# A four-layer hybrid network on one core: filter scaling and filtered copies moved to ScalarE, and the first scan unit written out by halves

## Chip, core and metric

The kernel is one program on one core of a Trainium2 chip. The metric is the device time of one execution in microseconds (us). The kernel before takes 3038.94 us, the median of three runs (3038.47 to 3039.41).

The engines are TensorE (PE in the profile; its weight loads are PEld), VectorE (DVE), ScalarE (ACT), GpSimd (POOL) and SyncE (SP), which issues most of the DMAs. Matmul results go to PSUM[...]. Everything here is float32; a 512-column product is two records of TensorE.

## What is computed

The input x has 8 images of 128 channels and 16 x 16 points, so 256 positions an image and 2048 positions in all. Four layers follow one another:

```python
x = x + adder2d(group_norm(x), W)                 # layer 0: minus the sum of |w - x| over 3x3 taps
# layer 1: three selective scans (forward, backward, sliced) over the positions
u, z  = split(layer_norm(x) @ in_proj.T)          # 256 channels each
uc    = silu(causal_conv1d(u, w4) + b)            # four taps
dt, Bm, Cm = split(uc @ xproj.T)                  # 8, 16 and 16 columns
delta = softplus(dt @ dtproj.T + db)
h_t   = exp(delta * A) * h_(t-1) + delta * uc * Bm   # 16 states a channel
y     = sum over states of h * Cm + uc * D
# ... attention between the three y, a gate with z, two 3x3 convolutions, + x
# layer 2: attention of one head, then a mixture of 8 experts (top 2)
# layer 3: 8 layers of linear attention and feed-forward, a tanh; then the spectral layer:
U_plus, U_minus = causal convolution of u (and of u with alternating sign) with 16 filters phi
out   = sum over k of sigma_k**0.25 * (U_plus[k] @ M_plus[k] + U_minus[k] @ M_minus[k])  + 3 taps of u @ M_u
```

The spectral layer is computed for four lengths of the sequence, weighted by a one-hot vector.

## The kernel before, in words

**Layer 0** (`adder_layer`, from line 303). For each of 128 filters and nine taps VectorE (line 419, 415) or ScalarE (421) makes a 128x2048 tile d, and TensorE sums it over channels with one-column selectors. The filters come in four groups of 32. After the last, `sums` (428) goes by four DMAs a group (430) to `total`, and four operations on VectorE (434) write X, the activations of layer 1, in four blocks of 512 positions. The tiles `x`, `w`, `pad`, `sh`, `sums` and `total` stand in one SBUF pool, "l0". The pools of layer 1 are laid over it, so a tile of layer 1 waits for what last used the bytes beneath it.

**Layer 1** (`_scans`, from 502). The work is cut into 12 units, each a pair of images (one block of 512 positions) and one of the three branches. A unit is prepared and then scanned. The preparation gives uc, delta, du = delta * uc and, through DRAM, the rows of B and C, each spread over the 128 partitions by DMA (`chunk`, 722). Channels come in two halves, h = 0 and 1. A scan runs over 16 states of a unit. For each state r and half: ScalarE makes the decay da (`decays`, 746; tiles da0 to da2 in three PSUM banks, number 2r + h modulo 3), GpSimd makes dbu = du * B (`inputs`, 736), VectorE scans (825) and multiplies both halves by C (836; for states 1 and 8 of a unit GpSimd does it, 834), and TensorE adds up the states in PSUM (acc). ScalarE first copies C to PSUM (`rows_of_c`, 741).

PSUM in this stage: three banks for da, one each with the tags "s", "f" and "cs", and two with the tag "acc".

The order of the loop over the states is written by hand (`tc.manual_schedule`, 808): the preparation of the next units (`prepare`, 646) and the work of `beside` (769) are mixed in by small steps. `first_unit` (668) prepares unit 0, when nothing else can run beside it, and stands outside of the hand-written order: a scheduler sorts its instructions. It normalises the block, projects it (two halves, pu), filters each half on TensorE with four products with diagonal matrices (pconv), makes the sigmoid from Exp, Ln and Exp, projects (pp), and for each half computes softplus: Abs and Relu, Exp, 1 + e to PSUM, Ln, and three operations on VectorE. Then du (713), the first dbu (739, on VectorE) and the first decays follow, and the first two steps of unit 1's preparation.

**Layers 2 and 3** (`performer_layer`, 1014). Four blocks of 512 positions go through 8 layers each; their steps are mixed by a table (`ORDER`) in a hand-written order. Blocks 0 and 1 run ahead of the others through layer 2 (`AHEAD`), beside the end of layer 1. `_block` (1393) is one block's way; at 1432 it adds the feed-forward to the state H, and `_squares` (1366) then squares H on ScalarE. Two sets of ScalarE tables alternate here (one with Ln and Exp, one with Gelu).

**The spectral layer.** `Spectral.__init__` (1662), called ahead of layer 2, loads the filter matrices T (16 of 128 x 258 columns) and scales all of them by sigma**0.25 with one operation on GpSimd (1673). `spectral_layer` (1711) takes two filters a step, in eight steps. VectorE makes the weighted matrices m (1706, 1708; two buffers, loaded by DMA); their sum and difference are me (1754 on VectorE, 1755 on GpSimd; two buffers). TensorE filters: 16 products p (two records each, three PSUM banks), each copied to ug by VectorE and ScalarE in turn:

```python
if n_evac % 2:
    nc.scalar.copy(dst, p4)          # line 1766
else:
    nc.vector.tensor_copy(dst, p4)   # line 1768
```

20 products g of me and ug then add to the result. All products are issued by the helper at line 279, all activations of layers 2 and 3 by the one at 1097, so groups are told apart by their tiles.

Of the kernel before, what the change touches and what calls it, by code (L numbers as in the profile page):

```python
# [16 lines left out]
P = 128  # L17
# [285 lines left out]
def adder_layer(E):  # L303
# [8 lines left out]
    with ExitStack() as ctx:  # L312
        p = ctx.enter_context(tc.tile_pool(name="l0", bufs=1))
        accp = ctx.enter_context(tc.tile_pool(name="l0acc", bufs=3))
        absp = ctx.enter_context(tc.tile_pool(name="l0abs", bufs=4))
        po = ctx.enter_context(tc.tile_pool(name="l0po", bufs=2, space=PSUM))
        ps = ctx.enter_context(tc.tile_pool(name="l0ps", bufs=2, space=PSUM))

        x = p.tile([P, B, L], F32, tag="x", name="x0")
        for b in range(0, B, 2):  # L320
            nc.sync.dma_start(x[:, b : b + 2, :], E.dram["x"][b : b + 2].rearrange("b c s -> c b s"))
        E.load_shared()
# [77 lines left out]


        sums = p.tile([P, NG, BLK], F32, tag="sums", name="sums")
        total = p.tile([P, NBLK, BLK], F32, tag="total", name="total")
        for g in range(NG):
            out = po.tile([P, BLK], F32, tag="o", name="o")
            for r in range(FG):
# [95 lines left out]
def _scans(E, ctx, F):  # L502
# [113 lines left out]
            E.mm(pp, w_x[:, k, h, :], uc[:, h, :], start=h == 0, stop=h == 1)  # L616
        return pp

    def softplus(k, s, h, proj, d, e, r, tag, gen):

        pd = ps.tile([P, UT], F32, tag=tag, name="pd")
        E.mm(pd, w_dt[:, k, h * P : (h + 1) * P], proj[0:DTR, :])
        yield 1
        yield LATER
        db = E.v("db" + s, h)
        nc.scalar.activation(e, pd, AF.Abs, bias=db)
        nc.scalar.activation(d, pd, AF.Relu, bias=db)
        yield LATER
        nc.scalar.activation(e, e, AF.Exp, scale=-1.0)
        one_e = ps.tile([P, UT], F32, tag=tag, name="one_e")  # L630
        nc.scalar.activation(one_e, e, AF.Identity, bias=E.ones[:, 0:1])
        yield LATER
        nc.vector.scalar_tensor_tensor(e, one_e, -1.0, e, ALU.add, ALU.subtract)
        nc.scalar.activation(r, one_e, AF.Ln)
        gen.tensor_sub(r, r, e)
        gen.tensor_add(d, d, r)

    def tiles():
        uc, delta, du = (two.tile([P, 2, UT], F32, tag=n, name=n) for n in ("uc", "delta", "du"))
# [6 lines left out]
    def prepare(k, s, p, got):  # L646
        new, pre, sig, proj = tiles()
        uc, delta = new["uc"], new["delta"]
        for h in range(2):
            pc = ps.tile([P, UB, L], F32, tag="s", name="pconv")  # L650
            yield from convolution(k, s, h, us[p], pc)
            yield LATER
            biased(s, h, pc, pre[:, h, :])
        yield from sigmoid(sig, pre)
        nc.gpsimd.tensor_mul(uc, pre, sig)
        yield LATER
        pp = projections(k, uc, proj, "s")
        yield 2
        yield LATER
        nc.scalar.copy(proj, pp)  # L660
        nc.sync.dma_start(new["rows"], proj[DTR:, :])
        got.update(new)
        for h in range(2):
            yield from softplus(k, s, h, proj, delta[:, h, :], pre[:, h, :], sig[:, h, :], "s", nc.gpsimd)
        yield LATER
        nc.gpsimd.tensor_mul(new["du"], delta, uc)

    def first_unit(k, s, p, got):

        src = E.X[:, blk(p)]  # L670
        pxc = ps.tile([P, UT], F32, tag="s", name="xc1")
        E.mm(pxc, E.center, src)
        rstd = one.tile([P, UT], F32, tag="ln_rstd", name="ln_rstd")
        nc.scalar.activation(rstd, pxc, AF.Square)
        var = ps.tile([P, UT], F32, tag="f", name="var1")
        E.mm(var, E.mean, rstd)
        nc.scalar.activation(rstd, var, AF.Ln, bias=E.eps)
        nc.scalar.activation(rstd, rstd, AF.Exp, scale=-0.5)
        t = xn[p] = two.tile([P, UT], F32, tag="xn", name="xn1")
        nc.vector.tensor_mul(t, pxc, rstd)  # L680
        nc.vector.tensor_scalar(t, t, E.v("ln_w"), E.v("ln_b"), ALU.mult, ALU.add)
        us[p] = two.tile([P, 2, UT], F32, tag="u", name="u1")
        tags = ("f", "s")
        for h in range(2):
            pu = ps.tile([P, UT], F32, tag=tags[h], name="pu")
            E.mm(pu, E.w["in_proj"][:, h * P : (h + 1) * P], t)
            (nc.vector.tensor_copy if h else nc.scalar.copy)(us[p][:, h, :], pu)
        for j, b in enumerate(BRANCHES):
            nc.scalar.activation(neg_a[:, j, :], E.vs("A" + b), AF.Exp)
        nc.vector.tensor_scalar_mul(neg_a, neg_a, -1.0)  # L690
        for d in das:
            nc.vector.memset(d[:, :, 0:1], 0.0)
        new, pre, sig, proj = tiles()
        uc, delta = new["uc"], new["delta"]
        for h in range(2):
            pc = ps.tile([P, UB, L], F32, tag=tags[h], name="pconv")
            for _ in convolution(k, s, h, us[p], pc):
                pass
            biased(s, h, pc, pre[:, h, :])
            for _ in sigmoid(sig[:, h, :], pre[:, h, :]):  # L700
                pass
            nc.vector.tensor_mul(uc[:, h, :], pre[:, h, :], sig[:, h, :])
        nc.scalar.copy(proj, projections(k, uc, proj, "f"))
        nc.sync.dma_start(new["rows"], proj[DTR:, :])
        parts = [
            softplus(k, s, h, proj, delta[:, h, :], pre[:, h, :], sig[:, h, :], tags[h], nc.vector) for h in range(2)
        ]
        for part in parts:
            next(part)
        for part in parts:  # L710
            for _ in part:
                pass
        nc.vector.tensor_mul(new["du"], delta, uc)  # L713
        got.update(new)


    units = [(k, s, p) for p in range(NPAIRS) for k, s in enumerate(BRANCHES)]
# [15 lines left out]
        c, j = divmod(n, CN)  # L733
        return got[i][name, c][:, j, :]

    def inputs(r, gen=nc.gpsimd):
        if r < states:
            dbs[r] = three.tile([P, 2, UT], F32, tag="db", name="dbu")
            gen.tensor_tensor(dbs[r], got[r // NST]["du"], bc(row("bs", r), 1, 2), ALU.mult)  # L739

    def rows_of_c(r):
        if r < states and r % NST not in AWAY:
# [46 lines left out]
            if p < NPAIRS - 2:  # L789
                yield from gates(p + 2)  # L790

    first_unit(*units[0], got[0])
    for c in range(2):
        chunk("bs", 0, c)
        chunk("cs", NST, c)
    for g in range(3):
        decays(g)
    inputs(0, nc.vector)
    inputs(1)
    rows_of_c(0)  # L800
    acc = late = None
    room = 0
    other = _Chain(beside())
# [589 lines left out]
def _block(S):  # L1393
# [23 lines left out]
    for i in range(NL):  # L1417
        sq = yield from _attention(S, i, h, sq, u, sums)
        w = S.layers[i]
        yield from _state_norm(S, h, sq, u)  # L1420
        g = one.tile([P, 4, BLK], F32, tag="g", name="g3")
        for f in range(0, 4, 2):
            p1 = [bank(S, [P, BLK], "p1") for _ in range(2)]
            for n in range(2):
                S.mm(p1[n], w["w1"][:, (f + n) * P : (f + n + 1) * P], u)
            for n in range(2):
                act(S, g[:, f + n, :], p1[n], AF.Gelu, bias=S.v(f"b1{i}", f + n))
            yield
        p2 = bank(S, [P, BLK], "p2")
        for f in range(4):  # L1430
            S.mm(p2, w["w2"][:, f * P : (f + 1) * P], g[:, f, :], start=f == 0, stop=f == 3)
        nc.vector.scalar_tensor_tensor(h, p2, S.added[f"b2{i}"], h, ALU.add, ALU.add)
        if i == NL // 2 - 1:
            yield
            pz = bank(S, [LAT, BLK], "pz3")
            S.mm(pz, S.enc, h)
            z = S.many.tile([P, BLK], F32, tag="t", name="z3")[0:LAT]
            act(S, z, pz, AF.Gelu, bias=S.v("enc_b")[0:LAT, :])
            yield
            ph = bank(S, [P, BLK], "ph2")  # L1440
            S.mm(ph, S.w["dec"], z)
            nc.vector.tensor_scalar_add(h, ph, S.added["dec_b"])
        if i + 1 < NL:
            sq = _squares(S, h)
            yield
            if S.t == 0:
                yield from _weights_of(S, i + 1)
# [211 lines left out]
class Spectral:  # L1659


    def __init__(self, E, ctx):
# [7 lines left out]
        self.H = pool.tile([P, NT], F32, tag="H", name="H")  # L1670
        self.u = pool.tile([P, B, TAPS - 1 + L], F32, tag="u", name="u4")
        nc.gpsimd.memset(self.u[:, :, 0 : TAPS - 1], 0.0)
        nc.gpsimd.tensor_tensor(self.T, self.T, bc(E.sg[:, :], 2, TW), ALU.mult)


        soft = pool.tile([P, 1, 4], F32, tag="soft", name="soft")
# [7 lines left out]
        nc.vector.tensor_sub(hot, hot, soft)  # L1684
        nc.vector.tensor_add(hot, hot, soft)
        self.hot = hot[:, 0, :]

    def take(self, E, t, xn, pt, dst):

# [21 lines left out]
def spectral_layer(E, W, out):  # L1711
# [8 lines left out]
    with ExitStack() as ctx:  # L1720
# [24 lines left out]
            a = tile[:]  # L1745
            return bass.AP(a.tensor, a.offset + offset, [list(a.ap[0]), *([s, n] for s, n in dims)])

        n_evac = 0
        for step in range(NK // KG):
            m = W.load(E, two, step)  # L1750
            W.running(E, [m[:, i].rearrange("p k s e -> p (k s e)") for i in range(4)])
# [6 lines left out]
            for b in range(B):  # L1758
                for q in range(2):
                    p4 = pu.tile([P, KG, 2, HL], F32, tag="u", name="p4")  # L1760

                    taps = at(W.T, step * KG * TW + 1, (TW, KG), (HL + 1 - q, 2), (1, HL))
                    E.mm(p4, ut[:, 2 * b + q, :], taps)
                    dst = at(ug, b * L + q * HL, (2 * NT, KG), (NT + (-HL if q else HL), 2), (1, HL))
                    if n_evac % 2:
                        nc.scalar.copy(dst, p4)  # L1766
                    else:
                        nc.vector.tensor_copy(dst, p4)  # L1768
                    n_evac += 1
            for k in range(KG):  # L1770
                for s in range(2):
                    for j, (i, lo, hi, b0, b1) in enumerate(groups):
# [61 lines left out]
```

## Time and profile before

| | us |
|---|---|
| median of three runs | 3038.94 |
| the profiled execution's own time | 3037.75 |
| its span, first to last instruction | 3036.0 |
| layer 0 (to the last d product) | 0 to 964 |
| first unit (to the first scan, L825) | 964 to 1004.75 |
| scans | 1004.75 to about 1700 |
| layer 1's end, layers 2 and 3 | about 1700 to 2790 |
| spectral layer | 2790 to 3036 |

The granted TensorE clock was 0.986 over the span. A line of the timeline has the start, the busy time, the engine, the program line, the operation with its tiles (out<-in) and shapes, the count, and in brackets how long the engine stood before it and what released it. A line of the waits has who waited, for whom, the total, the times and the longest. A line of the windows has the stretch, its length, then busy time and count of PE, PEld, DVE, ACT and POOL, the clock, the DMA share and GB/s. Instructions that overlap in an engine's pipeline are merged into one line, and a busy time can run into the next start.

### The profile page before, as it was taken

Reading aid. Unit: us, or ns where it says so; the run is one execution under the profiler, and the core shown is the slowest. Engines: PE = TensorE matmul, PEld = TensorE weight load, DVE = VectorE, ACT = ScalarE, POOL = GpSimd, SP = SyncE. Lnnn points to the kernel's source line nnn. Section 1 sums busy time; section 2 is a strip of 40 time slices with the busy share of each in tenths; the row PEclk is TensorE's granted clock in tenths of the full one; section 3 lists DMA queues with packets and bytes.
Section 4 is the critical chain, followed back from the end, with each engine's and each line's share of the span. In section 5 each row is a group of like instructions: output and inputs, shape, how many; then the busy total and the mean of one; then the engine's idle time right before and its main releaser. Section 6 shows DMA issues by size and latency. Waiting matters only on the chain.

```text
span 3036.0 us, 41650 instructions
## 1 busy us (share of the span) xinstructions
PE 2850.0 (94%) x16314; PEld 1258.5 (41%) x16314; DVE 2468.0 (81%) x3440; ACT 2228.8 (73%) x2664; POOL 732.1 (24%) x442
## 2 busy tenths in 40 slices
PE   6999999999998787998998998999999999999999
PEld 2222222222222233443443454455555655654444
DVE  6999999999997899999899657887777787784321
ACT  5999999999997777778777424577778778676111
POOL 3000000000000699998999400000000000000100
PEclk9999999999999999999999999999999999999999
DMA  1000000000000544444443200000000000001100
GB/s 41 1 2 5 2 1 5 1 1 5 2 1 5 166 142 150 133 148 144 134 156 136 86 28 1 14 1 14 14 14 1 14 14 1 14 1 52 42 28 14
DMA packets 39192, 131.47 MB, mean 43 GB/s; under 512 B 7490, under 2 KB 10572, under 8 KB 37588
## 3 DMA queue, kind: packets, MB, share of 16 engines
q1 hardware_dynamic: 38564, 128.02, 12.6%
q8 instruction: 128, 2.10, 0.3%
q10 hardware_dynamic: 432, 0.79, 0.1%
q14 instruction: 68, 0.56, 0.1%
HBM read 125.91 MB, written 1.84 MB: 42 GB/s over the span
## 4 chain that ended last, share of the span: by engine, by line
PE 68%; DVE 16%; ACT 7%; POOL 5%; issue 3%; DMA 1%; SPq 0%; DVEq 0%; ACTq 0%; POOLq 0%
PE o L279 30%; PE p L279 8%; PE acc L279 5%; DVE st L825 4%; PE g L279 4%; PE conv L279 4%; POOL dbu L739 2%; PE pc L279 2%; PE var L279 2%; PE pf L279 2%; PE pq L279 2%; PE pconv L279 1%; PE pa L279 1%; PE pn L279 1%; PE px L1584 1%
## 5 line engine op out<-in xcount | busy, mean ns | idle before, releaser
L279 PE MATMUL o<-d,sel 128*32 128x512 f32 x8512 | 922.8, 593 | 7.6 <-DVE d L419 5.5
L421 ACT ACTIVATE d<-sh,w 128x2048 f32<-128x2048 f32 x472 | 899.6, 1993 | 29.9 <-PE o L279 23.3
L419 DVE TENSOR_SCALAR d<-sh,w 128x2048 f32<-128x2048 f32 x592 | 724.5, 1292 | 13.5 <-PE o L279 10.4
L739 POOL TENSOR_TENSOR dbu<-du,bs 128x1024 f32<-128x1024 f32 x191 | 447.1, 2366 | 973.2 <-DVE du L713 970.9
L279 PEld LDWEIGHTS o<-d,sel 128*32 128x32 f32 x8512 | 274.3, 110 | 655.3 <-issue 533.0
L825 DVE TENSOR_TENSOR_SCAN st<-da,dbu 128x512 f32<-128x512 f32 x384 | 446.1, 1207 | 17.2 <-POOL dbu L739 15.1
L279 PE MATMUL acc<-st,cst 128*128 128x512 f32 x768 | 375.9, 621 | 57.3 <-DVE st L836 57.1
L752 ACT ACTIVATE da<-delta,neg_a 128x510 f32<-128x510 f32 x384 | 256.8, 684 | 79.0 <-DVE st L825 77.8
L279 PEld LDWEIGHTS acc<-st,cst 128*128 128x128 f32 x768 | 144.7, 196 | 256.2 <-issue 141.7
L836 DVE TENSOR_TENSOR st<-st,pcs 128x1024 f32<-128x1024 f32 x168 | 205.2, 1222 | 18.0 <-ACT pcs L744 0.9
L415 DVE SCALAR_TENSOR_TENSOR d<-sh,w,d 128x2048 f32<-128x2048 f32 x88 | 206.7, 2349 | 1.9
L1312 POOL TENSOR_TENSOR lw<-lw,turn 128x640 f32<-128x640 f32 x8 | 10.1, 1257 | 679.2 <-DVE turn L1311 586.3
L1089 ACT ACT_TABLE_LOAD x134 | 171.9, 1283 | 2.5
L1766 ACT COPY ug<-p 128x512 f32<-128x512 f32 x64 | 37.5, 585 | 181.9 <-PE p L279 181.9
L744 ACT COPY pcs<-cs 128x512 f32<-128x512 f32 x168 | 97.7, 582 | 55.2 <-DVE st L836 48.6
L279 PE MATMUL conv<-pad,f 128*128 128x512 f32 x288 | 135.0, 596 | 0.9 <-ACT pad L987 0.5
L279 PE MATMUL p<-un,lw 128*128 128x512 f32 x256 | 123.7, 605 | 3.8 <-DVE un L1383 2.1
L279 PE MATMUL p<-T,H 128*128 128x512 f32 x256 | 115.4, 603 | 6.1 <-DVE ug L1768 5.1
L279 PE MATMUL p<-g,lw 128*128 128x512 f32 x256 | 116.4, 597 | 3.9 <-ACT g L1097 3.9
L279 PE MATMUL g<-ug,me 128*128 128x512 f32 (+1 forms) x320 | 111.9, 509 | 0.0
L1097 ACT ACTIVATE ex<-ex 128x352 f32<-128x352 f32 x128 | 62.4, 493 | 51.6 <-DVE ex L1577 50.3
L279 PE MATMUL pf<-lw,rk 128*128 128x352 f32 x256 | 97.2, 476 | 0.5 <-DVE ek L1527 0.3
(347 smaller groups left out, 3943.0 us busy)
## 6 DMA issues: line engine op xcount, KB each, us to landing
bs<-rows SPq DMA_DIRECT2D x96, 512.0 KB, 3.8
cs<-rows SPq DMA_DIRECT2D x96, 512.0 KB, 4.7
m<-in_Mphi SPq DMA_DIRECT2D x8, 1024.0 KB, 4.8
lw<-in_layers SPq DMA_DIRECT2D x8, 948.0 KB, 4.5
f<-in_fuse SPq DMA_DIRECT2D x2, 1152.0 KB, 7.9
T<-in_T SPq DMA_DIRECT2D x1, 2064.0 KB, 7.6
x<-in_x SPq DMA_DIRECT2D x4, 256.0 KB, 7.4
total<-sums SPq DMA_DIRECT2D x16, 64.0 KB, 2.0
```

Of the source, the lines that this page charges most:

```text
L279: self.nc.tensor.matmul(out, lhsT=lhsT, rhs=rhs, start=start, stop=stop)
L415: nc.vector.scalar_tensor_tensor(d, tap(k), wk, d, ALU.max, ALU.add)
L419: nc.vector.tensor_scalar(d, tap(k), wk, None, ALU.max)
L421: nc.scalar.activation(d, tap(k), AF.Abs, scale=-1.0, bias=wk)
L739: gen.tensor_tensor(dbs[r], got[r // NST]["du"], bc(row("bs", r), 1, 2), ALU.mult)
L744: nc.scalar.copy(pcs[r], row("cs", r))
L752: nc.scalar.activation(das[g % 3][:, :, 1:], d[:, :, 1:], AF.Exp, scale=a)
L825: nc.vector.tensor_tensor_scan(st[:, h, :], da, dbs[r][:, h, :], 0.0, ALU.mult, ALU.add)
L836: nc.vector.tensor_tensor(st, st, bc(pcs[r][:, :], 1, 2), ALU.mult)
L1089: S.tc.keep_in_program_order(S.nc.scalar.preload_act_table_set(name))
L1097: S.nc.scalar.activation(out, src, func, **kw)
L1766: nc.scalar.copy(dst, p4)
```

## The change

It has three parts.

1. **First unit.** `x` and `total` of layer 0 get a pool of their own, `l0last`. `first_unit` becomes a generator within a hand-written order. Half 1 is filtered on VectorE, straight from the PSUM bank of its projection, by one tensor_scalar and three scalar_tensor_tensor; half 0 stays on TensorE, and its sigmoid starts from PSUM (Exp with the bias `less`). 25 products of the identity with itself (`spare`, in bank "acc") are put between the products of the unit. The softplus has its maximum on VectorE and 1 + e in SBUF. du and the first dbu are made by halves. The copy of u for half 1 comes last.
2. **Filter matrices.** The operation on GpSimd goes. While block 0 runs through its 8 layers, ScalarE scales two of the 16 matrices a layer, right after line 1432.
3. **Filtered signals.** All copies of p to ug are ScalarE's.

```diff
-        x = p.tile([P, B, L], F32, tag="x", name="x0")
+        x = last.tile([P, B, L], F32, tag="x", name="x0")
...
-        total = p.tile([P, NBLK, BLK], F32, tag="total", name="total")
+        total = last.tile([P, NBLK, BLK], F32, tag="total", name="total")
...
-    def first_unit(k, s, p, got):
+    def first_unit(k, s, p, new, pre, sig, proj):
+        spare = ps.tile([P, P], F32, tag="acc", name="spare")
+        def meanwhile(n):
+            for _ in range(n):
+                E.mm(spare, ident, ident)
...
+        meanwhile(9)
         pxc = ps.tile([P, UT], F32, tag="s", name="xc1")
-        E.mm(pxc, E.center, src)
+        E.mm(pxc, E.center, E.X[:, blk(p)])
...
+        meanwhile(1)
         var = ps.tile([P, UT], F32, tag="f", name="var1")
...
+        meanwhile(8)
...
+        for h, tag in ((1, "s"), (0, "f")):
+            pus[h] = ps.tile([P, UT], F32, tag=tag, name="pu")
+            E.mm(pus[h], E.w["in_proj"][:, h * P : (h + 1) * P], t)
+        nc.scalar.copy(us[p][:, 0, :], pus[0])
+        nc.vector.tensor_scalar(p1, u1, E.v("cw" + s, 7), E.v("cb" + s, 1), ALU.mult, ALU.add)
+        for m in range(1, 4):
+            o = p1[:, :, m:]
+            nc.vector.scalar_tensor_tensor(o, u1[:, :, : L - m], E.v("cw" + s, 7 - m), o, ALU.mult, ALU.add)
+        meanwhile(2)
...
+        nc.scalar.activation(t, pc, AF.Exp, scale=-1.0, bias=less)
+        nc.vector.tensor_scalar_add(pre[:, 0, :], pc, E.v("cb" + s, 0))
...
+        meanwhile(1)
+        E.mm(pp, w_x[:, k, 1, :], uc[:, 1, :], start=True, stop=False)
+        meanwhile(3)
+        E.mm(pp, w_x[:, k, 0, :], uc[:, 0, :], start=False, stop=True)
+        nc.scalar.copy(proj, pp)
+        nc.sync.dma_start(new["rows"], proj[DTR:, :])
+        yield
+        meanwhile(1)
...
+        for h, (pd, d, e, r, one_e) in enumerate(halves):
+            nc.scalar.activation(e, pd, AF.Abs, bias=db)
+            nc.scalar.activation(e, e, AF.Exp, scale=-1.0)
+            nc.vector.tensor_scalar(d, pd, db, 0.0, ALU.add, ALU.max)
+        for pd, d, e, r, one_e in halves:
+            nc.vector.tensor_scalar_add(one_e, e, 1.0)
+            nc.scalar.activation(r, one_e, AF.Ln)
+            nc.vector.scalar_tensor_tensor(e, one_e, -1.0, e, ALU.add, ALU.subtract)
+        for h, (pd, d, e, r, one_e) in enumerate(halves):
+            nc.vector.tensor_sub(r, r, e)
+            nc.vector.tensor_add(d, d, r)
+            nc.vector.tensor_mul(new["du"][:, h, :], d, uc[:, h, :])
+            yield
+        nc.scalar.copy(us[p][:, 1, :], pus[1])
+        yield
...
+        for h in range(2):
+            next(first)
+            nc.vector.tensor_mul(dbs[0][:, h, :], new["du"][:, h, :], row("bs", 0))
+            decays(h)
+            if h == 0:
+                rows_of_c(0)
+        inputs(1)
+        next(first)
+        decays(2)
...
         nc.vector.scalar_tensor_tensor(h, p2, S.added[f"b2{i}"], h, ALU.add, ALU.add)
+        if S.t == 0:
+            for k in range(i * NK // NL, (i + 1) * NK // NL):
+                S.spectral.scale(S, k)
...
-        nc.gpsimd.tensor_tensor(self.T, self.T, bc(E.sg[:, :], 2, TW), ALU.mult)
...
+    def scale(self, E, k):
+        E.nc.scalar.activation(self.T[:, k, :], self.T[:, k, :], AF.Copy, scale=E.sg[:, k : k + 1])
...
-                    if n_evac % 2:
-                        nc.scalar.copy(dst, p4)
-                    else:
-                        nc.vector.tensor_copy(dst, p4)
-                    n_evac += 1
+                    nc.scalar.copy(dst, p4)
```

In the built program the order of the instructions on each engine differs from the one before in these three places, and otherwise by a few neighbouring products on TensorE that change places. On VectorE the scan of state 0, half 0, comes between the subtraction and the addition of half 1. On ScalarE the order there is: decay of half 0, the copy of C, decay of half 1, the copy of u for half 1, and the decays for state 1, half 0 and half 1, and for state 2, half 0; then the bias of unit 1's first filtered half (pre), and only then the decay for state 2, half 1.

## The prediction

> **What bounds the kernel now.** I read the page first, for the engine that is never idle.
>
> ```profile
> PE 2850.0 (94%) x16314; PEld 1258.5 (41%) x16314; DVE 2468.0 (81%) x3440; ACT 2228.8 (73%) x2664; POOL 732.1 (24%) x442
> ```
>
> TensorE (PE) is busy for 94% of 3036.0 us, so a gain has to come from the few places where it stands, or from the scan stage (about 1005 to 1700), where VectorE is the busy one. The change touches three places, so I took the timeline of each. First the start of the scans (columns: start, busy time, engine, line, operation, and in brackets the idle time before it and what ended it):
>
> ```profile
> 967.40 1.73 PE L279 MATMUL xc<-X,center 128*128 128x512 f32 x2 [3.52 <-DVE X L434]
> ...
> 970.33 0.58 ACT L674 ACTIVATE ln_rstd<-xc 128x512 f32<-128x512 f32 x1
> ...
> 970.96 2.07 PE L279 MATMUL var<-ln_rstd,mean 128*128 128x512 f32 x2 [1.83 <-ACT ln_rstd L674]
> ...
> 974.46 0.69 DVE L680 TENSOR_TENSOR xn<-xc,ln_rstd 128x512 f32<-128x512 f32 x1 [3.19 <-ACT ln_rstd L678]
> ...
> 975.83 3.75 PE L279 MATMUL pu<-xn,w_in_proj 128*128 128x512 f32 x4 [2.79 <-issue]
> ...
> 979.38 8.02 PE L279 MATMUL pconv<-u,diag 128*128 128x512 f32 x16
> ...
> 984.02 0.69 ACT L603 ACTIVATE pre<-pconv,vecs 128x512 f32<-128x512 f32 x1 [5.52 <-PE pconv L279]
> ...
> 992.07 0.58 ACT L703 COPY proj<-pp 40x512 f32<-40x512 f32 x1 [1.87 <-PE pp L279]
> ...
> 1004.75 2.34 DVE L825 TENSOR_TENSOR_SCAN st<-da,dbu 128x512 f32<-128x512 f32 x2
> ...
> 1007.12 1.22 DVE L836 TENSOR_TENSOR st<-st,pcs 128x1024 f32<-128x1024 f32 x1
> 1007.75 0.67 ACT L603 ACTIVATE pre<-pconv,vecs 128x512 f32<-128x512 f32 x1
> ...
> 1009.51 0.69 ACT L752 ACTIVATE da<-delta,neg_a 128x510 f32<-128x510 f32 x1 [1.09 <-DVE st L825]
> ```
>
> This is one serial chain, nothing beside it: from 967.40 to 1004.75 each engine waits for the previous one. From 1007 on VectorE runs without idle time until about 1058. Second, the change of stage, where the filter matrices are scaled:
>
> ```profile
> 1815.32 7.07 POOL L1673 TENSOR_TENSOR T<-T,sg 128x4128 f32<-128x4128 f32 x1 [7.61 <-DMA T<-in_T]
> 1815.39 7.06 DVE L1233 TENSOR_TENSOR ex<-ex 128x32 f32<-128x32 f32 x1
> 1823.73 7.92 PE L279 MATMUL pe<-lw,u 128*128 128x512 f32 x12 [8.49 <-DVE y L1248]
> ```
>
> A 128x32 product takes 7.06 us, exactly as long as GpSimd's (POOL's) T; its twin L1232, just before, took 0.18. TensorE stands behind it for 8.49 us. Third, the spectral stage:
>
> ```profile
> 2821.50 9.60 PE L279 MATMUL p<-T,H 128*128 128x512 f32 x22
> 2832.01 4.89 PE L279 MATMUL p<-T,H 128*128 128x512 f32 x10 [0.91 <-DVE ug L1768]
> 2836.74 14.00 PE L279 MATMUL g<-ug,me 128*128 128x512 f32 x40
> ...
> 2937.79 13.90 PE L279 MATMUL p<-T,H 128*128 128x512 f32 x32
> ```
>
> In five of the eight steps the filtering products wait for a copy (ug) on VectorE; VectorE had stood 1.69 us at L1706 for the DMA of m, with copies queued behind.
>
> [...] 0.18 became 7.06. [...] xc after 3.52 us idle takes 1.73, the same product at 1017.74 takes 1.02. [...] the copies at L1510 need no load.
>
> **First unit, part by part.** Durations are of the row named; 0.03 us is the usual hand-over.
> - Removed wait: ScalarE's L674 waited for all of X (970.05), since its buffer lay on x's. x and total move to a pool of their own. Square then starts when xc ends.
> - Clock: 25 spare products. Nearest row: 128x128 products at 1837.69, 8 records in 1.06, so 0.25 us for one (two records). Nine are 2.2 us in the 3.52 us gap, eight 2.0 us beside Ln, Exp and xn (2.8 us): costing nothing, as the gaps are the cover. They could cost 25 x 0.25 = 6.2 us with no gap. I take the fast clock.
> - New times: xc 967.40 to 968.42; Square to 969.03; var 1.13 to 970.15; Ln, Exp (0.69, 0.63) to 971.54; xn ready 972.84; pu starts 972.90, before 975.83: 2.9 gained.
> - Then pu for h=1 ready at 974.0, for h=0 at 974.9. h=1 is filtered by four VectorE operations (0.72 each) to 976.9 while h=0 is copied (0.58) and filtered on TensorE (8 records of 0.43) to 979.1. Sigmoid of h=1 (2.05) ends at 979.0, of h=0 (three steps, 2.1) at 981.25, uc 981.97, pp 983.1, proj 983.70. Before, 992.65: another 6.0 gained, 8.95 in all.
> - proj to the first L836: before 14.5. Now pd h=0 985.2 (behind a spare and an acc product), Abs, Exp, Abs, Exp to 987.85. VectorE's second max waits for the second Abs (987.2) and delays the first 1+e: Ln at 988.4. From there VectorE alone: e, 1+e, e, subtract, add, du, dbu, subtract, scan, add, du, dbu, scan, about 0.65 each and 1.2 a scan: first L836 at 998.1. 14.4: nothing gained. Gain so far 1007.12 - 998.1 = 9.0.
> - DMAs: rows, bs, cs follow proj on SP as before; bs landed 5.5 after proj, now 989.2, needed at 992.4. GpSimd's dbu for state 1 starts at 996.3 beside a two-input dbu of VectorE (0.69), as before, and is due at 999.3: just in time.
> - New wait: u of h=1 is copied last (ScalarE, 996.2 to 996.8) and frees bank "s" for the second unit's convolution. TensorE, idle since 987, is slow again: 5.95 us as at 1000.74, so to 1002.8. ScalarE's pre stands in order ahead of the decay for state 2, h=1. That decay is ready at 1004.1 where the scan wants it at 1002.85: 1.3 lost. Before, pre had no wait. Sum of the unit: 9.0 - 1.3 = 7.7 (bounds 5.0 and 10.0).
>
> The scan loop behind is a fixed order with VectorE as bound, so the 7.7 are carried on.
>
> **Filter matrices.** The product on GpSimd goes: 7.06 - 0.18 = 6.9 on VectorE. TensorE then doesn't go cold: its first two pe products took 3.77 at 1823.73, 1.72 when warm, of which VectorE stood 1.5 for. I take 1.3 of it: 8.2 (bounds 6.9 and 8.6). Sixteen ScalarE pieces of 128x258 come in, two per layer of block 0. No row shows them; nearest L1003, 128x256 in 0.42. A pair is 0.84. In the built order seven pairs stand ahead of an operation for which ScalarE waits anyway:
>
> ```profile
> ACT lsq L1097 <- DVE H L1432: 16.0, 20, 1.8
> ```
>
> The gaps there (six such Squares and one qp) are 1.79, 0.85, 0.67, 1.11, 1.22, 1.05 and 1.20; the eighth pair, ahead of a table load, has none. Left over 0.17 + 0.82: cost 1.0. Bounds: 0 and 16 x 0.42 = 6.7; it can't gain. Behind them stand the other blocks' activations, and TensorE is full:
>
> ```profile
> 2100.00:2250.00 150.00, 146.67 (x851) 86.06 (x850) 116.20 (x291) 115.20 (x181) 2.97 (x6) 0.99 0.02 7
> ```
>
> (TensorE 146.67 of 150), so a delay there is a loss. Net of part two: 7.2.
>
> **Spectral copies.** A step with the wait has 2836.74 - 2821.50 = 15.24 for p, one without 13.74. The four steps exceed by 1.50, 1.49, 1.57, 1.41; the first (its own wait 1.44) I take at 1.5. Sum 7.5 (bounds 5.1, the sum of TensorE's waits, and 8.0). Cover: a ScalarE copy is 0.58 (L1766), a product pair comes every 0.86, three banks. VectorE keeps only m and me, wanted two steps later; what is late next is TensorE itself.
>
> **Sum.** 7.7 + 7.2 + 7.5 = 22.4. Against the profiled execution's own 3037.75 that is 3015.3; the median shown is 1.2 higher, so 3016.5.
>
> **Rivals.**
> - Spare products don't hold the clock (the gaps between them stay): xc +0.71, var +0.94, pu +1.75, convolution +1.7: 5.1 lost, 3021.6. For: 1.3 us gaps remain. Against: products at 993 ran fast among gaps of 2 us.
> - The sixteen pieces cost their full time as TensorE is full: +5.7, 3022.2. Against: the gaps above.
> - The matrix chain m, me ends the spectral waits instead: 7.5 not gained, 3024.0. Against: VectorE waits up to 14 us for g before me.
> - Slower: ScalarE becomes the bound of the spectral stage. It decides from 16 copies a step over 13.73 us, 0.86 a copy; all gains are gone at 13.73 + 22.4/8 = 16.5, 1.03 a copy. If copy and release don't overlap, 2 x 0.58 = 1.16: 8 x (18.56 - 13.73) = 38.6 more, 3055. Against: copies on both engines now release banks in time.
> - Better than computed: the second convolution costs no stall and the parts reach their upper bounds, near 3010.
>
> **How the numbers follow.** Forecast 0.70 (own range 3012.5 to 3020), slow clock 0.10, pieces 0.08, matrix chain 0.05, better 0.05, slower 0.02. The range 3011.5 to 3022.5 takes in the first three. Within 0.2% (6.1 us, about what a measurement can tell) 0.01 from the tails; slower 0.02; faster 0.97.
>
> **What would show it.** xc and var at 1.0 to 1.1 us; the first L836 near 998; a ScalarE wait for pconv near 999 to 1003, and an idle VectorE of about 1.3 before the second scan of the third state; L1233 at 0.18 and no TensorE wait of 8 us near 1807; p of all spectral steps near 13.7. Wrong if performer stretches grow by more than 2 us, or spectral waits move to another releaser.

## The result, and the profile after

The changed kernel took 3015.41 us, the median of four runs (3011.62 to 3019.29), beside 3038.70 for four runs of before: ratio 0.9924, 95% interval 0.9907 to 0.9941. A second set of five runs gave 3016.16 beside 3040.65: 0.9922 (0.9910 to 0.9935). The forecast was 3016.5, 22.4 less than before; 23.3 and 24.5 came.

The profiled execution of after was its longest run, 3019.29, with a span of 3017.5. Lines have moved: the multiply by C is now L889 (836 before), the scan L878 (825), softmax's twin product L1286 (1233), the copy of p L1824 (1766 and 1768), the matrix pieces L1745. The page still shows TensorE as the bound:

```profile
PE 2848.3 (94%) x16356; PEld 1263.0 (42%) x16356; DVE 2426.0 (80%) x3387; ACT 2270.8 (75%) x2739; POOL 724.3 (24%) x441
```

VectorE lost 42 us of work and ScalarE gained 42, but these sums don't show the gain: it is 18.5 us of span, found in three places. Here and below, lines of a timeline that are left out are marked by three dots. Timeline of the first unit:

```profile
963.79 2.27 PE L279 MATMUL spare<-cst 128*128 128x128 f32 x18
...
967.37 1.13 PE L279 MATMUL xc<-X,center 128*128 128x512 f32 x2 [1.31 <-DVE X L436]
...
968.54 0.60 ACT L693 ACTIVATE ln_rstd<-xc 128x512 f32<-128x512 f32 x1 [7.09 <-PE xc L279]
...
969.19 1.12 PE L279 MATMUL var<-ln_rstd,mean 128*128 128x512 f32 x2 [0.47 <-ACT ln_rstd L693]
...
973.06 1.98 PE L279 MATMUL pu<-xn,w_in_proj 128*128 128x512 f32 x4 [0.96 <-DVE xn L702]
...
983.41 0.58 ACT L732 COPY proj<-pp 40x512 f32<-40x512 f32 x1 [1.87 <-PE pp L279]
...
997.28 5.82 PE L279 MATMUL pconv<-u,diag 128*128 128x512 f32 x8 [9.35 <-ACT u L757]
...
998.80 1.22 DVE L889 TENSOR_TENSOR st<-st,pcs 128x1024 f32<-128x1024 f32 x1
...
1003.14 0.69 ACT L605 ACTIVATE pre<-pconv,vecs 128x512 f32<-128x512 f32 x1 [3.65 <-PE pconv L279]
...
1004.44 1.22 DVE L878 TENSOR_TENSOR_SCAN st<-da,dbu 128x512 f32<-128x512 f32 x1 [1.05 <-ACT da L796]
```

xc takes 1.13 instead of 1.73 and var 1.12 instead of 2.07: TensorE kept its clock (granted 1.00 over both, where before had 0.61 and 0.50). The first L889 stands 8.3 ahead of before's L836. The last three lines are the new wait: u freed its bank late, the convolution took 5.82 at a mean granted clock of 0.63, ScalarE stood 3.65 for it, and the decay queued behind came 1.05 late. Timeline of the change of stage:

```profile
1812.93 0.18 DVE L1286 TENSOR_TENSOR ex<-ex 128x32 f32<-128x32 f32 x1
...
1814.39 3.18 PE L279 MATMUL pe<-lw,u 128*128 128x512 f32 x6 [1.61 <-DVE y L1301]
```

7.06 us became 0.18, and TensorE's wait 1.61 instead of 8.49; the granted clock over the first 3 us of pe behind it was 1.00, where before had 0.50. Timeline of the spectral stage:

```profile
2795.20 14.00 PE L279 MATMUL g<-ug,me 128*128 128x512 f32 x40
2809.03 13.90 PE L279 MATMUL p<-T,H 128*128 128x512 f32 x32
2822.77 14.00 PE L279 MATMUL g<-ug,me 128*128 128x512 f32 x40
2836.61 13.90 PE L279 MATMUL p<-T,H 128*128 128x512 f32 x32
```

From 2809.03 to 2822.77 are 13.74 us: no p line waits for a copy any more (the very first one stands 0.78 for H, as it did before). ScalarE's groups there (busy, mean ns of one, idle ahead of it):

```profile
L1824 ACT COPY ug<-p 128x512 f32<-128x512 f32 x128 | 75.0, 586 | 136.6 <-PE p L279 136.6
L1745 ACT ACTIVATE T<-T,sg 128x258 f32<-128x258 f32 x16 | 7.2, 496 | 0.0
```

ScalarE waits for TensorE, not the other way.

Marks along the two traces, before minus after (the change of stage is the start of softmax's twin product): 7.2 at the 16th scan, 4.1 at the last scan, 2.5 at the change of stage, 10.8 at the first p, 18.5 at the end. So 4.7 of the first unit's gain had gone by the end of layer 1, in code that the change leaves alone. That was the open question.

### The profile page after: what moved, and what is told of

Its sections match the earlier page's. It is cut to its first block, busy times and chain, and to the rows that moved or that the text cites. A ratio compares the mean times of both kernels' runs of the same rounds, so it can differ in the third digit from the quotient of the medians.

```text
span 3017.5 us, 41743 instructions
## 1 busy us (share of the span) xinstructions
PE 2848.3 (94%) x16356; PEld 1263.0 (42%) x16356; DVE 2426.0 (80%) x3387; ACT 2270.8 (75%) x2739; POOL 724.3 (24%) x441
## 4 chain that ended last, share of the span: by engine, by line
PE 70%; DVE 15%; ACT 8%; POOL 3%; issue 2%; DMA 0%; DVEq 0%; ACTq 0%; POOLq 0%
PE o L279 30%; PE p L279 10%; PE acc L279 5%; DVE st L878 5%; PE g L279 4%; PE conv L279 3%; PE pc L279 2%; PE var L279 2%; PE pf L279 2%; PE pconv L279 2%; PE pq L279 2%; POOL dbu L783 1%; ACT da L796 1%; PE pn L279 1%; PE pa L279 1%
## 5 line engine op out<-in xcount | busy, mean ns | idle before, releaser
L878 DVE TENSOR_TENSOR_SCAN st<-da,dbu 128x512 f32<-128x512 f32 x384 | 446.3, 1207 | 18.0 <-POOL dbu L783 14.0
L889 DVE TENSOR_TENSOR st<-st,pcs 128x1024 f32<-128x1024 f32 x168 | 205.2, 1222 | 18.2 <-DVE st L878 0.5
L1824 ACT COPY ug<-p 128x512 f32<-128x512 f32 x128 | 75.0, 586 | 136.6 <-PE p L279 136.6
```

The costliest lines, as they stand in the source:

```text
L878: nc.vector.tensor_tensor_scan(st[:, h, :], da, dbs[r][:, h, :], 0.0, ALU.mult, ALU.add)
L889: nc.vector.tensor_tensor(st, st, bc(pcs[r][:, :], 1, 2), ALU.mult)
```

## Experiments

In all of them "before" ran beside the kernel on the same chip, and its median moved from 3034 to 3041 between sets, so I compare ratios and, for causes, lengths in the traces.

**The three parts, one at a time.** p1 is after without parts 2 and 3, p2 is before with part 2 alone, p3 before with part 3 alone. The edits against before:

```diff
 p2
+        if S.t == 0:
+            for k in range(i * NK // NL, (i + 1) * NK // NL):
+                S.spectral.scale(S, k)
...
-        nc.gpsimd.tensor_tensor(self.T, self.T, bc(E.sg[:, :], 2, TW), ALU.mult)
...
 p3
-                    if n_evac % 2:
-                        nc.scalar.copy(dst, p4)
-                    else:
-                        nc.vector.tensor_copy(dst, p4)
+                    nc.scalar.copy(dst, p4)
```

p1: 

> Part 1 alone (first unit and the pool l0last; filter matrices scaled on GpSimd and copies on both engines as before). Theory: the first unit gives 7.2 us at the 16th scan, and these are carried to the end: 3038.7 - 7.2 = 3031.5. Rival: the 4 to 5 us that the traced run of after gave back between the scans and the end of layer 1 belong to the change of the first unit and come every time: 3036. The scans' offset against before, scan by scan, should be about -7.2 at the 16th; if the give-back is chance, the steps at which it comes differ from those of after (about scans 220, 250 and 355).

p2: 

> Part 2 alone (matrices scaled by ScalarE in sixteen pieces). Theory: 8.2 gained at the change of stage, pieces of 0.50 us hidden in ScalarE's waits: 3038.7 - 8.2 = 3030.5. Rival: pieces cost as forecast (1.0): 3031.5, or in full (16 x 0.50 = 8.0): 3038.5. In the profile the 128x32 product at 0.18 us and the stretch from the performer's start to the first p of the spectral layer shorter by 8.2.

p3: 

> Part 3 alone (all copies of p to ug on ScalarE). Theory: 7.6 gained, 3031.1; spectral stage 238 us in place of 245.6 and every p window 13.7. Rival: with the GpSimd scaling still there and the load of the matrices unchanged nothing differs, so the gain is the same; if instead part of the 7.6 came from the earlier end of other parts, 2 to 4 us less: 3034.

| | median, us | before beside it | ratio, 95% interval |
|---|---|---|---|
| p1 | 3029.07 | 3036.83 | 0.9979 (0.9972 to 0.9986) |
| p2 | 3032.98 | 3036.83 | 0.9984 (0.9976 to 0.9991) |
| p3 | 3028.63 | 3036.83 | 0.9974 (0.9963 to 0.9985) |

Medians: 7.8, 3.9 and 8.2 less, 19.8 together where the whole gave 23.3. p1 and p3 are as expected; p2 is 4 us short. The traces answer the open question. Start of scans against before (plus is later):

| | 16th scan | last scan | change of stage |
|---|---|---|---|
| after | -7.2 | -4.1 | -2.5 |
| p1 | -7.7 | -8.5 | -6.9 |
| p2 | +0.5 | +3.5 | +5.1 |
| p3 | -0.7 | +1.9 | +3.6 |

p1 has the first unit of after and gives back under 1 us; p2 and p3 have before's first unit and scans, and lose 4.6 and 4.3 in the same stretch. The loss isn't the change's: the same code varies by some 4 us from run to run.

**What varies.** The traces record TensorE's granted clock; it is whole or half (1.00 or 0.50 below). Windows of after around layer 2's last po2e (the products that sum up the experts), cut at the record's own steps:

```profile
1936.88:1940.29 3.41, 1.28 (x6) 0.45 (x4) 3.38 (x9) 2.27 (x4) 0.00 (x0) 1.00 0.00 0
1940.29:1943.70 3.41, 3.41 (x10) 1.91 (x9) 1.75 (x5) 0.69 (x1) 0.00 (x0) 0.50 0.22 31
1943.70:1947.12 3.42, 3.03 (x22) 1.83 (x22) 0.91 (x2) 0.27 (x1) 0.00 (x0) 0.50 0.61 253
```

First PE busy time, third from the end the clock. In the first window TensorE worked 1.28 of 3.41 us, as it waits 2.13 for ScalarE; then two windows at half clock. In every one of the fourteen traces all half-clock stretches, but a last one that the end of the trace cuts off, are 3.41 us or multiples and start on one grid of 3.413 us; the grid's phase is the same from layer 1 to the end of a trace and differs from trace to trace (a step at 967.78 us in before, at 967.49 in after). I cut all fourteen traces by their grids, from 960 us to the end: after a window at whole clock with TensorE busy for under 0.4 of it, half clock followed 135 times of 135; from 0.4 to 0.5, 21 of 82; above, 42 of 7906 (19 of these in two windows where about half of the records are products of 34 columns). From half clock it came back only after a window busy for 0.8 or more (31 times of 31 in the traces of before and after). So a gap of 2.13 us, shorter than a window of 3.41, is enough when it falls into one. Whether it does differs from run to run: in p1 the same gap of 2.13 stands ahead of po2e and no half clock follows (two records in 1.12, where after took 1.93).

What a half-clock window costs depends on where it falls. From the 16th scan to the last, p1 and p3 both have 41.0 us at half clock, yet take 679.8 and 683.1 us. From the last scan to the change of stage no trace has any half clock. Still, this stretch takes 106.4 us in the six traces with two half-clock windows in the last 40 us of the scans (after, p1, p2, p3, nospare, nopiece) and 104.7 in the eight without: in the six TensorE enters it with four products of a convolution left over, in the eight with none. This is 1.6 of the 4.7 that after lost against before. Another 2.2 of it lie in the last 44 scans (83.3 us against 81.1), where the places of the windows differ as well. For the rest I show no cause.

**After again, without the spare products, without the pieces, and with more spare products.**

```diff
 nospare
-                E.mm(spare, ident, ident)
+                pass
...
 nopiece
-        if S.t == 0:
-            for k in range(i * NK // NL, (i + 1) * NK // NL):
-                S.spectral.scale(S, k)
...
 ucopy
         nc.sync.dma_start(new["rows"], proj[DTR:, :])
+        nc.scalar.copy(us[p][:, 1, :], pus[1])
...
-        nc.scalar.copy(us[p][:, 1, :], pus[1])
 fillonly (fill: this and ucopy)
     po = bank(S, [P, BLK], "po2e")
+    if S.t == 2:
+        for _ in range(7):
+            S.mm(po[:, 0:P], ident, ident)
...
     pl = bank(S, [P, P], "pl3")
+    FILLED.append((FILLED[-1] + 1) % 32 if FILLED else 0)
+    for _ in range({6: 5, 10: 2, 22: 2, 27: 3, 31: 4}.get(FILLED[-1], 0)):
+        S.mm(pl, ident, ident)
```

after2: 

> The changed kernel again, to have it beside the others and a second profile of it. In the traces so far TensorE drops to half clock only for stretches of 3.41 us or multiples, all starting on one grid of 3.413 us; the grid's phase against the program differs from run to run. Theory: that phase decides which of the same short gaps of TensorE are followed by half clock, and this makes the scatter. So the gaps must be the same as in the first profile of after and the starts again on one grid with another phase; the single runs between 3007 and 3021, the lower the higher their mean clock. Rival: the scatter comes from elsewhere (DMA); then two runs of one mean clock differ by as much as any two.

nospare: 

> After without the 25 spare products. Theory: the gaps of 1.3 to 3.5 us between the unit's products stay, TensorE is at half clock again from about 968 on: xc 1.7 us in place of 1.13, pu 3.7 in place of 1.98, pconv slower; the first multiply by C about 4 to 5 us later than after's 998.8, and the time 4 to 5 us longer. Rival: the shorter chain (Square no longer waits) leaves gaps short enough, and the clock holds without the products: no more than 1 us.

nopiece: 

> After without the sixteen ScalarE pieces, so that the filter matrices are not scaled at all (left out: the factors sigma**0.25). Theory: the pieces cost nothing, same as after within 1 us, and the stretch from xc of layer 3's start to the first p of the spectral layer is as long as in after when the stretches at half clock are equal (970.5). Forecast's own value: 1.0 less; the rival of the pieces in full: 8.0 less (16 x 0.50).

ucopy: 

> After, with the copy of u for half 1 of the first unit moved to right behind the copy of proj, where ScalarE stood 2.07 us for pd. It frees bank s 11 us earlier, so unit 1's first convolution runs right behind pd. Theory: the stall of 1.05 us before the second scan of the third state goes, and TensorE stays warm: 1 us less than after, 3014.4, and the offset of the 16th scan is -8.2. Rival: another wait (dbu, the copy of C) takes its place: 3015.4, the stall there with another releaser. Slower rival: the copy delays Abs and Exp by its 0.58: 3016, first multiply by C near 999.4.

fill: 

> The earlier copy of u, and besides 23 spare products in six gaps of TensorE in layers 2 and 3 that were followed by half clock in some of the traces (7 ahead of the last po2e, 2.13 us; 16 ahead of five of the 32 pl groups, where TensorE stands 0.91 to 1.69 us for sqq). Theory: half clock no longer follows there (four stretches, 13.6 to 17 us at half clock in the profile of after, worth 6.8 to 8.5 us; in a mean run somewhat less): 3 to 7 us less than after, median near 3010, and a smaller scatter. Rival: the products fit the gaps but the other gaps trip in their place: same as after. Slower rival: they delay the products behind them by their 23 x 0.21 = 4.9 us: after + 5.

fillonly: 

> After with the 23 spare products in layers 2 and 3 alone, the copy of u where after has it. The run with both was 7.4 us below after. Theory: nearly all of it is the spare products (the stretch from xc to the first p at 964.3 us, no half clock in it), since the earlier copy of u gave 16.0 against 16.2: ratio 0.990 to 0.991, some 7 us below after. Rival: the two need each other; then within 2 us of after, ratio 0.992.

| | median, us | before beside it | ratio, 95% interval |
|---|---|---|---|
| after2 | 3016.16 | 3040.65 | 0.9922 (0.9910 to 0.9935) |
| nospare | 3023.97 | 3040.65 | 0.9941 (0.9927 to 0.9955) |
| nopiece | 3014.66 | 3040.65 | 0.9924 (0.9911 to 0.9936) |
| fill | 3008.79 | 3040.65 | 0.9902 (0.9888 to 0.9915) |
| ucopy | 3016.00 | 3036.83 | 0.9932 (0.9918 to 0.9946) |
| fillonly | 3009.49 | 3038.30 | 0.9905 (0.9889 to 0.9922) |

Clock and time go together in after2: 3009.36 at a mean clock of 0.993, 3014.82 to 3018.83 at 0.988 or 0.989. The mean clock doesn't account for all of the scatter: two runs of nopiece at 0.989 took 3012.69 and 3019.30. Within one stage the tie is close; it can be read from the stretch between xc at the start of layer 3 and the first p of the spectral layer, in all traces without GpSimd's scaling:

| half clock in it, us | length of the stretch, us |
|---|---|
| 0 | 964.3 (fill), 964.1 (fillonly) |
| 3.41 | 965.5 (ucopy) |
| 10.24 | 968.6 (after2), 968.5 (twocopy), 968.8 (poolback) |
| 13.65 | 970.5 (after), 970.8 (p2) |
| 20.48 | 973.3 (nospare), 973.3 (nopiece) |

From first to last row 9 us are lost for 20.5 at half clock, 0.44 for one. nopiece lies on this line with the others: the sixteen pieces cost nothing that can be seen (nospare, which has them, is 0.1 shorter). Timeline of ScalarE in after, around the first and the third pair of pieces:

```profile
1925.19 0.90 ACT L1745 ACTIVATE T<-T,sg 128x258 f32<-128x258 f32 x2
1927.07 0.63 ACT L1150 ACTIVATE lsq<-H 128x512 f32<-128x512 f32 x1 [0.98 <-DVE H L1485]
...
2177.14 0.90 ACT L1745 ACTIVATE T<-T,sg 128x258 f32<-128x258 f32 x2
2177.95 0.62 ACT L1150 ACTIVATE lsq<-H 128x512 f32<-128x512 f32 x1
```

A pair takes 0.90 us. Behind the first ScalarE still waits 0.98 for H, behind the third not at all.

The windows of fill over the same po2e:

```profile
1933.57:1936.98 3.41, 2.84 (x20) 2.15 (x19) 3.38 (x7) 2.27 (x4) 0.00 (x0) 1.00 0.00 0
1936.98:1940.40 3.42, 3.03 (x28) 1.88 (x29) 2.51 (x8) 0.95 (x2) 0.00 (x0) 1.00 0.40 102
```

Busy 2.84 of 3.41 and the clock stays at 1.00: seven spare products (14 records in 1.72 us) do for layer 2 what 25 do for the first unit. In fill and fillonly no half clock is left from layer 2 to the last product. After's stretch at 2779.97 is gone too, though no spare product stands there; it is missing in five of the unfilled traces as well. Both kernels with them beat after, by 7.4 us in the set shared with after2 and by 5 to 6 by fillonly's ratio; they are the fastest that I ran. That the two don't need each other is settled by fillonly: the earlier copy of u adds nothing outside the scatter. That scatter, which was to become smaller, did not: 7.9 and 7.4 us from the lowest to the highest of four runs, against 7.7 in the first four runs of after.

nospare went the way of the rival in which the clock is not held. Its timeline of TensorE:

```profile
966.56 2.07 PE L279 MATMUL xc<-X,center 128*128 128x512 f32 x2 [3.52 <-DVE X L436]
969.32 2.07 PE L279 MATMUL var<-ln_rstd,mean 128*128 128x512 f32 x2 [0.69 <-ACT ln_rstd L693]
974.14 3.78 PE L279 MATMUL pu<-xn,w_in_proj 128*128 128x512 f32 x4 [2.75 <-DVE xn L702]
978.60 6.03 PE L279 MATMUL pconv<-u,diag 128*128 128x512 f32 x8 [0.68 <-ACT u L708]
```

The gap of 3.52 is back, and xc, var, pu and the convolution take 2.07, 2.07, 3.78 and 6.03 in place of 1.13, 1.12, 1.98 and 3.68. Its first multiply by C came at 1003.49, 4.7 later than after's, and a stall of 1.53 followed. So of the first unit's gain about 5 is the spare products'. From pu to the end of proj it took 15.08, where after took 10.93 and before 16.82: the new way of filtering and the other edits of this piece leave 1.7 without the clock. They were not run apart.

ucopy's stall did go, but another took its place. VectorE's timeline:

```profile
999.26 4.56 DVE L878 TENSOR_TENSOR_SCAN st<-da,dbu 128x512 f32<-128x512 f32 x4
...
1013.68 1.22 DVE L878 TENSOR_TENSOR_SCAN st<-da,dbu 128x512 f32<-128x512 f32 x1 [0.26 <-ACT da L796]
...
1017.60 1.22 DVE L878 TENSOR_TENSOR_SCAN st<-da,dbu 128x512 f32<-128x512 f32 x1 [0.23 <-ACT da L796]
```

The four scans of the second and third state run through; then the decay is late twice, since unit 1's preparation now reaches ScalarE earlier. From proj to the 16th scan 1.05 us is lost against before, 1.4 to 1.5 in after's two traces. The expected 1 us is 0.3 to 0.45 there, and nothing in the medians.

**Without part 2, with the pool as before, and with every copy twice.**

```diff
 p13
...
+        nc.gpsimd.tensor_tensor(self.T, self.T, bc(E.sg[:, :], 2, TW), ALU.mult)
-        if S.t == 0:
-            for k in range(i * NK // NL, (i + 1) * NK // NL):
-                S.spectral.scale(S, k)
...
 poolback
-        x = last.tile([P, B, L], F32, tag="x", name="x0")
+        x = p.tile([P, B, L], F32, tag="x", name="x0")
...
-        total = last.tile([P, NBLK, BLK], F32, tag="total", name="total")
+        total = p.tile([P, NBLK, BLK], F32, tag="total", name="total")
 twocopy
                     nc.scalar.copy(dst, p4)
+                    nc.scalar.copy(dst, p4)
```

p13: 

> Parts 1 and 3 without part 2 (the filter matrices are scaled on GpSimd as before). Part 2 alone gave 3.9 us in the medians where its stretch in the trace gave 7.9 to 8.5. Theory: the 8 us are real and the small median of part 2 alone is a chance of the half-clock stretches elsewhere; then this kernel is 8 us slower than after, near 3023.5 to 3024. Rival: something takes half of part 2 back every time; then 4 us slower, 3019.5.

poolback: 

> After with x and total in pool l0 again. Theory: a tile of the first unit lies on x's bytes, so Square (ln_rstd from xc) waits until the fourth X is written, near 970.0 where it started near 968.5: 1.5 us later up to the projection, and the time 1.5 us longer, 3017. Rival: the layout puts nothing that is early on x's bytes: same as after. Slower rival: the wait opens a gap of over 2 us ahead of var and TensorE goes to half clock: 3 to 5 us.

twocopy: 

> After with every copy of p to ug done twice on ScalarE (the second writes the same values). It prices the slower rival: copies that take 1.17 us each. 16 copies a step are 18.8 us where TensorE needs 13.74: each p stretch about 18.6 to 18.8, and 8 x 4.9 = 39 us more, 3055. If copies overlap in ScalarE's pipeline, less: at 0.86 us a pair nothing is lost.

| | median, us | before beside it | ratio, 95% interval |
|---|---|---|---|
| p13 | 3021.77 | 3033.97 | 0.9957 (0.9944 to 0.9971) |
| poolback | 3017.00 | 3033.97 | 0.9946 (0.9932 to 0.9960) |
| twocopy | 3026.43 | 3033.97 | 0.9975 (0.9965 to 0.9985) |

p13 is 0.0035 above after2, some 10 us, where p2 alone had given 5 by its ratio. Both are loose; the trace is not: the stretch from xc to the first p is 978.45 with 13.65 us of half clock besides that of the change of stage, after's with the same 970.48, and p1 and p3 (976.7 with 10.24) stand against after2's 968.6. Part 2 is worth 8.0 or 8.1 each time. Why p2's runs showed only half of it is not fully settled. Their mean clock rose by 0.0007 over before's, where the 10.24 us of half clock saved at the change of stage alone would give 0.0017; this fits an unlucky draw of other gaps.

poolback held the slower rival. Its timeline:

```profile
968.36 0.75 DVE L435 SCALAR_TENSOR_TENSOR X<-x,wall,total 128x512 f32<-128x512 f32 x1 [0.62 <-DMA total<-sums]
...
969.52 0.58 ACT L692 ACTIVATE ln_rstd<-xc 128x512 f32<-128x512 f32 x1
...
970.15 2.07 PE L279 MATMUL var<-ln_rstd,mean 128*128 128x512 f32 x2 [2.42 <-ACT ln_rstd L692]
...
972.01 3.62 PE L279 MATMUL spare<-cst 128*128 128x128 f32 x16
```

Square waits for the last X again, TensorE stands 2.42, and this time half clock follows (var takes 2.07 in place of 1.12), so the spare products themselves take 3.62 in place of 1.95 and stand in the way of pu. proj came 2.6 and 3.5 later than in after's two traces. In this trace the pool is worth more than its 1 us of waiting because it keeps that gap short. By its ratio it is worth some 7 us, with 4 us of uncertainty on either kernel; the traces show no more than 3.5. That the median is the 3017 of the theory is luck, as before ran near 3034 in this set.

twocopy lost 10 us in the spectral stage of its trace, not 39. Its TensorE:

```profile
2803.21 4.54 PE L279 MATMUL p<-T,H 128*128 128x512 f32 x10
2808.10 2.84 PE L279 MATMUL p<-T,H 128*128 128x512 f32 x6 [0.34 <-ACT ug L1825]
2811.25 2.84 PE L279 MATMUL p<-T,H 128*128 128x512 f32 x6 [0.30 <-ACT ug L1825]
2813.93 1.02 PE L279 MATMUL g<-ug,me 128*128 128x512 f32 x2
2814.78 4.54 PE L279 MATMUL p<-T,H 128*128 128x512 f32 x10
2819.17 13.06 PE L279 MATMUL g<-ug,me 128*128 128x512 f32 x38
2832.06 4.54 PE L279 MATMUL p<-T,H 128*128 128x512 f32 x10
```

A step is 28.85 (2803.21 to 2832.06) in place of 27.58 (2809.03 to 2836.61 in after), and the stage 247.9 in place of 237.7. Two copies take 1.06: ScalarE does the 32 of a step in 16.94 us without a pause. But the built order moved g products in between the p, and three banks let copies lag a little, so the time that ScalarE lacks is partly spent beside g. The forecast's threshold took the 13.74 of the p stretch as all the time there is. By its ratio (0.9975, after2's 0.9922) twocopy lost some 16 us; for what goes beyond the 10 I have no cause.

## Why the prediction was right, step by step

- **First unit up to pu:** forecast 2.9, measured 2.8 (975.83 to 973.06). Pu to the end of proj: 6.0, measured 5.9 (16.82 became 10.93). Softplus to the first multiply by C: 0, measured 0.3 lost. Together 8.3 instead of 9.0. The reasons hold: nospare and poolback each bring back the gap that they were to bring back. That small products in the gaps would keep the clock was an estimate of mine, which the trace of before doesn't show; after and nospare show it (var in 1.12 and 2.07).
- **New wait:** forecast 1.3, measured 1.05 (0.78 in after2), with the releaser and the queue that were named. Net 7.2 (16th scan; 8.2 in the second trace) against 7.7.
- **Filter matrices:** 8.2 forecast; after's stretch from xc to the first p is 8.3 shorter than before's at equal half clock besides the change of stage.
- **Pieces: the step that failed.** Forecast 1.0, measured nothing (nopiece). The price was nearly right: a pair takes 0.90, since the second piece starts 0.40 behind the first, where 0.84 was forecast. A single one lasts 0.496 us in the trace, where the forecast took 0.42. The cover was right too: behind five pairs ScalarE still waits 0.25 to 0.98, behind the second, the third and the eighth at most 0.05. What failed is the step from there: that a delay of ScalarE is a loss because TensorE is full. The stretch came out no longer for the sixteen pieces. That ScalarE's work behind a pair is due at once was argued, not shown; which slack took it up stays open.
- **Spectral copies:** forecast 7.5, measured 7.7 (245.5 became 237.8 in the traces, and 243.6 against 236.1 in p1 and p3). The forecast's sum has no load of ScalarE's tables for these copies or the pieces, and none came: 136 loads before and after.
- **Sum:** 22.4 against 23.3. In the profiled pair alone it was 18.5, since 4.7 was lost in layer 1. At least 3.8 of that lies in stretches whose length goes with the place of the half-clock windows. The range of 11 us was about what chance alone does to this kernel, so that the median came within 1.1 us of the forecast is in part luck.
- **Rivals.** Slow clock: refuted, and priced rightly (5.1; nospare 4.7 at the first multiply). One argument against it was misread: the gap shortly ahead of the products at 993 was one of 1.30 (at 990.98), not of 2 us. Matrix chain: no wait of its kind. Slower: mis-priced, 39 where doubling the copies cost 10 in the stage, or 16 by the ratio. What the forecast didn't have is that in these traces the clock changes window by window (3.41 us), so that one execution's profile is a draw.

## What to carry to other kernels

Fill the short gaps of TensorE with small products where the clock matters: here they cost nothing that can be seen where they fit the gap, and gained time (4.7 us at the first multiply with the 25 of the first unit, 5 to 7 with the 23 of layers 2 and 3), though not a smaller scatter. A difference of a few us between two profiles is a cause only when the same difference stands in the stretch that was changed; count the half-clock windows first. An operation beside which another engine's takes longer (0.18 us became 7.06 beside GpSimd's 7.07) is dear by what stands behind it: here one GpSimd product cost 8 us and its sixteen pieces elsewhere nothing.

## What was not expected of the hardware

- Half clock came in windows of 3.41 us on a grid whose phase changes from run to run. A gap of 2.13 us tripped it in each trace that was not filled except p1 and p3, two of 0.92 us among products of 34 columns in most, and the same gaps passed in others.
- Half clock costs 0.44 us per us in the TensorE-bound stage, a little under the 0.50 that work on TensorE alone would lose (an estimate from the granted clock of 0.50).
- Back-to-back ScalarE copies of 0.586 us overlap: two take 1.06 (twocopy, 32 in 16.94).
